# A two-layer graph network on one core: the second layer's products move into the tile of the gathered features, with two such tiles instead of four

## The chip, the cores and the metric

The kernel runs on one core of a Trainium2 chip. The metric is the device time of one execution in microseconds (us), the median of several runs. A difference of about 0.2% is what a measurement of this kernel can tell from none.

## What is computed

The reference takes 6250 nodes with 128 features and 206,250 directed edges sorted by their target node (`dst`). The first layer is a graph attention layer with a feed-forward block; the second, which the change is about, is an equivariant convolution. Cut to what matters, the second layer is:

```python
f0 = x0 @ W1_0e / sqrt(32);  f1 = einsum('nui,uw->nwi', x1, W1_1o) / sqrt(32)
e0, e1 = feat0[edge_src], feat1[edge_src]          # gather by source node
h = gelu(edge_scalar_attr @ W_mlp1 / sqrt(8));  h = gelu(h @ W_mlp2 / sqrt(64))
out0_a = (h @ Wp_00) * e0 * ea0
out0_b = (h @ Wp_11) * sum(e1 * ea1) / sqrt(3)
out1_a = (h @ Wp_01) * e0 * ea1
out1_b = (h @ Wp_10) * e1 * ea0
n0, n1 = segment_sum(concat(out0_a, out0_b)), segment_sum(concat(out1_a, out1_b))   # by dst
y = cos * self + sin * (n0 @ W2_0e, n1 @ W2_1o);   x = layernorm(x + y)
```

Everything is in float32. The output is the 6250 x 128 node table after both layers.

## The kernel before

The edges are cut into tiles of 128 (one edge to a partition), six tiles (TU) make a unit of 768 edges, and there are 269 units. Because edges are sorted, a unit's targets lie in a window of 32 nodes, so its sum over edges is a matmul of the edge values with a one-hot matrix of width 32, and the result is added into an accumulator in SBUF at the unit's first node.

The first layer (`attention`) walks through the units; GpSimd (POOL) gathers one 128-row tile of a node table per instruction (`gather`, line 366), six to a unit. Its output goes into a DRAM table `FEAT` (features for the second layer) and `BASE`.

The second layer is `convolution`, line 746. It works on pairs of units (135 pairs, 134 of two units and one of one), and each pair in three chunks (c = 0, 1, 2), each of two tiles from either unit, so of four edge tiles. The order of the instructions on each engine is the order in which the Python code issues them; waits between engines follow from the buffers. The steps:

- `load(p)`, line 775: SyncE starts the transfers of the edge attributes (`e8` for eight pairs at once, `e4` for each pair).
- `fetch(p)`, line 785: twelve gathers from `FEAT` into the tile `f` of the pair, 128 partitions x 12 x 128 floats. There are four such buffers. The six tiles of the first unit come first, then those of the second; tile t of unit i lies in slot 2t + i, so chunk c reads slots 4c to 4c + 3.
- `radial(p, k)`, line 791: one of the two small dense layers per edge on TensorE (line 801), with a gelu on ScalarE (line 802). It runs two pairs ahead.
- `filters(p, c)`, line 804: the four weights of each edge, on TensorE into PSUM (line 808), two chunks ahead.
- `products(p, c)`, line 810, all on VectorE: `oh`, the one-hot of the targets (line 817); `os`, the one-hot times the four edge attributes (line 823); `vy`, the features times the weights in two versions j, in one multiplication at line 828 and two at line 832. `os` and `vy` come from a pool with two buffers each.
- `sums(p, c)`, line 838: for each of the four edge tiles two matmuls into the PSUM tile `y` of the pair, with `vy` as the weights and `os` as the moving operand (lines 849 and 851).
- `collect(p)`, line 853: VectorE adds `y` to the accumulator, once for each unit (line 859).
- `nodes.step` advances `finish` (line 889) in groups of two blocks of 128 nodes: 16 matmuls (line 908), VectorE and ScalarE work for the norm (`moments`, lines 620 to 623; `norm`, lines 629 to 632), and the store of the output.

The main loop, line 869, goes over steps q = 3p + c. In each: on c = 0 `load(p + 2)` and `fetch(p + 2)`; then `products` of chunk q, `collect` of the pair before on c = 1, `sums` of chunk q - 1, `filters` of chunk q + 2, a `radial` of pair p + 2, and a step of `finish`. In this layer GpSimd has no other instruction than the gathers, after clearing the accumulator at the start (line 761). Before a gather may write into a buffer of `f`, the products of the pair that used it four pairs ago must be done.

Of the kernel before, what the change touches and what calls it, by code (L numbers as in the profile page):

```python
# [8 lines left out]
F32 = mybir.dt.float32  # L9
# [7 lines left out]
P = 128  # L17
D = 128
# [16 lines left out]
TU = 6  # L35
# [72 lines left out]
class Fast:  # L108
# [637 lines left out]
    def convolution(self):  # L746


        tc, nc, a, NU = self.tc, self.nc, self.a, self.NU
        NPR, CT = -(-NU // 2), 2  # L750
        PARTS = TU // CT
        with ExitStack() as st:
            def pool(n, b, **k):
                return st.enter_context(tc.tile_pool(name=n, bufs=b, **k))
            cw, ld, wk = pool("fcw", 1), pool("fcl", 3), pool("fck", 2)
            hp, wp, yp = pool("fhp", 2, space=PSUM), pool("fwp", PARTS, space=PSUM), pool("fyp", 1, space=PSUM)

            acc = cw.tile([P, 4, self.NX], F32, name="acc4")
            step = -(-self.NX // 4)
            for x in range(0, self.NX, step):  # L760
                nc.gpsimd.memset(acc[:, :, x:min(x + step, self.NX)], 0.0)
            nodes = Queue(self.finish(st, yp, acc), self.done)
            m1 = cw.tile([P, EB, P], F32, name="m1")
            nc.scalar.dma_start(m1, a["m1"])
            m2 = cw.tile([P, P], F32, name="m2")
            nc.scalar.dma_start(m2, a["m2"])
            wq = cw.tile([P, 2 * D], F32, name="wq")
            nc.scalar.dma_start(wq, a["wq"])
            fs, e8s, e4s, hs, h1s, ws, vys, ys = {}, {}, {}, {}, {}, {}, {}, {}
            NQ = PARTS * NPR  # L770

            def units(p):
                return min(2, NU - 2 * p)

            def load(p):
                if p % EB == 0:
                    g = min(EB, NPR - p)
                    e8 = ld.tile([P, UE], F32, name="e8", bufs=2)
                    nc.sync.dma_start(e8[:g * 16], a["e8t"][p:p + g].rearrange("g k e -> (g k) e"))
                    for i in range(g):  # L780
                        e8s[p + i] = e8[:g * 16], m1[:g * 16, i]
                e4s[p] = ld.tile([P, 2 * TU, 4], F32, name="e4", bufs=4)
                nc.sync.dma_start(e4s[p], a["e4t"][:, p * 2 * TU:(p + 1) * 2 * TU, :])

            def fetch(p):
                f = fs[p] = ld.tile([P, 2 * TU, D], F32, name="f", bufs=4)
                for i in range(units(p)):
                    for t in range(TU):
                        self.gather(f[:, 2 * t + i, :], self.FEAT, 2 * p + i, t)

            def radial(p, k):


                if k == 0:
                    (x, m), sc = e8s.pop(p), 1.0 / math.sqrt(8.0)
                else:
                    x, m, sc = h1s.pop(p), m2, 1.0 / 8.0
                h = (h1s, hs)[k][p] = wk.tile([P, UE], F32, name=f"h{k}")
                for s in (slice(0, UE // 2), slice(UE // 2, UE)):
                    ps = hp.tile([P, UE // 2], F32, name="h_ps")  # L800
                    nc.tensor.matmul(ps, m, x[:, s], start=True, stop=True)  # L801
                    nc.scalar.activation(h[:, s], ps, AF.Gelu_apprx_tanh, scale=sc)  # L802

            def filters(p, c):
                w = ws[p, c] = wp.tile([P, 2 * CT, D], F32, name="w")
                for t in range(CT):
                    e = (c * CT + t) * P
                    nc.tensor.matmul(w[:, 2 * t:2 * t + 2, :], hs[p][:, e:e + P], wq, start=True, stop=True)  # L808

            def products(p, c):  # L810
                m = units(p)
                own = slice(0, 2 * CT, 3 - m)
                at = slice(2 * CT * c, 2 * CT * (c + 1), 3 - m)
                n = m * CT
                f, w = fs[p][:, at], ws.pop((p, c))[:, own]
                oh = wk.tile([P, CT, 2, W], F32, name="oh")
                nc.vector.tensor_tensor(  # L817
                    oh[:, :, :m],
                    self.l[:, 2 * p:2 * p + m, c * CT:(c + 1) * CT].rearrange("p u t -> p t u")[:, :, :, None]
                    .to_broadcast([P, CT, m, W]),  # L820
                    self.iota[:, None, None, :].to_broadcast([P, CT, m, W]), op=OP.is_equal)
                os = wk.tile([P, 2 * CT, 4, W], F32, name="os")
                nc.vector.tensor_mul(  # L823
                    os[:, own], oh.rearrange("p t u w -> p (t u) w")[:, own, None, :].to_broadcast([P, n, 4, W]),
                    e4s[p][:, at, :, None].to_broadcast([P, n, 4, W]))

                vy = wk.tile([P, 2 * CT, 2, D], F32, name="vy")
                nc.vector.tensor_mul(  # L828
                    vy[:, own, :, :32], w[:, :, :64].rearrange("p t (j x) -> p t j x", j=2),
                    f[:, :, None, :32].to_broadcast([P, n, 2, 32]))  # L830
                for j in range(2):
                    nc.vector.tensor_mul(  # L832
                        vy[:, own, j, 32:].rearrange("p t (c x) -> p t c x", c=3),
                        w[:, :, None, 64 + j * 32:96 + j * 32].to_broadcast([P, n, 3, 32]),
                        f[:, :, 32:].rearrange("p t (c x) -> p t c x", c=3))
                vys[p, c] = os, vy

            def sums(p, c):


                m = units(p)
                os, vy = vys.pop((p, c))
                if c == 0:
                    ys[p] = yp.tile([P, 2, 4, W], F32, name="y", bufs=2)
                for t in range(CT):
                    for i in range(m):
                        e = 2 * t + i
                        last = c == PARTS - 1 and t == CT - 1 and i == m - 1
                        nc.tensor.matmul(ys[p][:, i, 0], vy[:, e, 0], os[:, e, 3],  # L849
                                         start=(c == t == i == 0), stop=False)  # L850
                        nc.tensor.matmul(ys[p][:, i, 1:], vy[:, e, 1], os[:, e, :3], start=False, stop=last)  # L851

            def collect(p):
                y = ys.pop(p)
                for i in range(units(p)):
                    u = 2 * p + i
                    r = nc.vector.value_load(self.r0[0:1, u:u + 1], min_val=0, max_val=self.n)  # L857
                    v = acc[:, :, bass.ds(r, W)]
                    nc.vector.tensor_add(v, v, y[:, i])  # L859

            for p in range(min(2, NPR)):
                load(p)
                fetch(p)
                radial(p, 0)
                radial(p, 1)
            for q in range(2):
                filters(q // PARTS, q % PARTS)

            for q in range(NQ + PARTS):
                p, c = q // PARTS, q % PARTS  # L870
                if c == 0 and p + 2 < NPR:
                    load(p + 2)
                    fetch(p + 2)
                if q < NQ:
                    products(p, c)
                if c == 1 and p:
                    collect(p - 1)
                if 0 < q <= NQ:
                    sums((q - 1) // PARTS, (q - 1) % PARTS)
                if q + 2 < NQ:  # L880
                    filters((q + 2) // PARTS, (q + 2) % PARTS)
                if c != 1 and p + 2 < NPR:
                    radial(p + 2, c // 2)
                if p:
                    nodes.step(min(2 * p, NU) - 1)
            nodes.rest()
# [746 lines left out]
```

## Time and profile before

| | us |
|---|---|
| median of 3 runs | 4422.91 (4422.65 to 4431.17) |
| profiled execution, its own time | 5622.66 |
| its span, first to last instruction | 5620.2 |
| first `f` gather starts, last one starts | 2820.9, 5574.1 |
| POOL busy; `f` gathers, `xl` gathers | 3239.3; 1543.2, 1651.8 |
| PE busy; weight loads | 3763.6; 2955.2 |
| VectorE busy, ScalarE busy | 2550.7, 951.4 |
| mean granted clock of TensorE | 0.742 of full speed |

The page of the profile gives the busy time of each engine (PE is TensorE's matmuls, PEld its weight loads, DVE VectorE, ACT ScalarE, POOL GpSimd, SP SyncE). A group of instructions is a line of the code, an engine, an operation and the tiles, out<-in, with the count, busy us, mean ns of one, the engine's idle time before it and what ended most of that. A wait named "issue" is time in which an engine waited for nothing that the profile shows. A row of the timeline is start, duration, engine, line, operation, tiles and count, and in brackets the idle time before and its releaser. The second layer is about the second half of the profiled span. The profiled execution is longer than the runs that are timed, so its shares are not those of the timed runs.

### The profile page before, as it was taken

The page shows a single profiled execution, that of the slowest core. Times are in us where ns is not written, and L with a number is a line of the kernel's source. Part 1 is how long each engine was busy: PE and PEld are TensorE (multiplying, and loading weights), DVE is VectorE, ACT ScalarE, POOL GpSimd, SP SyncE. Part 2 cuts the span into 40 slices and gives each one's busy share as a digit, 9 for nine tenths or more (in the row PEclk, how much of TensorE's full clock was granted, in tenths as well). Part 3 has the DMA queues.
Part 4 walks back from the last instruction along what each step waited for, and adds up shares of the span by engine and source line. Part 5 has one row for each costly group of instructions (what it writes and reads, how often), then busy time and mean ns, then how long its engine had stood idle before and what let it go on. Part 6 is the DMA issues. An engine that isn't in the chain of part 4 may idle for free. (4 is left out here: it accounts for less than half of the span.)

```text
span 5620.2 us, 66997 instructions
## 1 busy us (share of the span) xinstructions
PE 3763.6 (67%) x21381; PEld 2955.2 (53%) x21381; DVE 2550.7 (45%) x6023; ACT 951.4 (17%) x2528; POOL 3239.3 (58%) x3236
## 2 busy tenths in 40 slices
PE   3566667667767676666656767767766766676667
PEld 2455555555555555545534555555555655555556
DVE  1465555656655656655623333333333333333334
ACT  1111212222221222212301111111111111111111
POOL 6256666666666666664255555555555555655553
PEclk6677777777777777776767777777777777777778
DMA  4444344334443444433111111111111111111111
GB/s 118 133 117 110 106 108 117 107 105 119 115 110 107 113 112 112 111 100 100 41 50 44 44 47 43 46 42 44 46 46 44 44 46 42 47 46 46 46 43 32
DMA packets 290616, 428.21 MB, mean 76 GB/s; under 512 B 122700, under 2 KB 199454, under 8 KB 290254
## 3 DMA queue, kind: packets, MB, share of 16 engines
q0 software_dynamic: 103296, 218.27, 15.9%
q1 hardware_dynamic: 183258, 197.74, 11.8%
q10 hardware_dynamic: 3700, 7.82, 0.4%
q8 instruction: 173, 2.83, 0.2%
q14 instruction: 189, 1.55, 0.1%
HBM read 403.55 MB, written 19.96 MB: 75 GB/s over the span
## 5 line engine op out<-in xcount | busy, mean ns | idle before, releaser
L366 POOL DMA_INDIRECT f<-fFEAT,fsrc x1614 | 1543.2, 956 | 1225.6 <-DVE oh L817 620.4
L366 POOL DMA_INDIRECT xl<-fXL,fsrc x1590 | 1651.8, 1039 | 989.4 <-issue 422.5
L823 DVE TENSOR_TENSOR os<-oh,e 128x512 f32<-128x512 f32 x405 | 280.3, 692 | 1543.1 <-remote 689.6
L851 PE MATMUL y<-os,vy 128*128 128x96 f32 x3228 | 794.6, 324 | 249.4 <-issue 247.6
L849 PEld LDWEIGHTS y<-os,vy 128*128 128x128 f32 x3228 | 590.5, 214 | 398.0 <-issue 267.3
L849 PE MATMUL y<-os,vy 128*128 128x32 f32 x3228 | 588.8, 260 | 275.4 <-issue 225.8
L420 PE MATMUL z<-fw,ea 128*128 128x136 f32 x3228 | 661.5, 351 | 137.3 <-issue 63.1
L851 PEld LDWEIGHTS y<-os,vy 128*128 128x128 f32 x3228 | 562.7, 214 | 248.3 <-issue 247.3
L420 PEld LDWEIGHTS z<-fw,ea 128*128 128x128 f32 x3228 | 561.2, 244 | 205.5 <-issue 117.3
L802 ACT ACTIVATE h<-h_ps 128x384 f32<-128x384 f32 x540 | 259.4, 490 | 2415.4 <-remote 985.3
L808 PE MATMUL w<-wq,h 128*128 128x256 f32 x1620 | 549.7, 456 | 113.3 <-issue 99.4
L538 PE MATMUL m<-xl,oh 128*32 128x136 f32 x3228 | 267.5, 352 | 272.3 <-issue 98.2
L808 PEld LDWEIGHTS w<-wq,h 128*128 128x128 f32 x1620 | 329.1, 223 | 196.7 <-issue 167.8
L832 DVE TENSOR_TENSOR vy<-w,f 128x384 f32<-128x384 f32 (+1 forms) x810 | 408.3, 545 | 0.0
L801 PE MATMUL h_ps<-e,m 128*128 128x384 f32 (+1 forms) x540 | 265.2, 624 | 202.4 <-ACT h L802 172.0
L551 PEld LDWEIGHTS m<-fcst,sb 128*128 128x128 f32 x1076 | 193.0, 237 | 341.7 <-issue 159.0
L551 PE MATMUL m<-fcst,sb 128*128 128x32 f32 x1076 | 183.4, 302 | 210.5 <-ACT sb L543 109.1
L423 PE MATMUL z<-xl,fcst 128*128 128x408 f32 x538 | 306.5, 655 | 13.7 <-issue 12.5
L538 PEld LDWEIGHTS m<-xl,oh 128*32 128x32 f32 x3228 | 132.9, 127 | 340.4 <-issue 141.8
L801 PE MATMUL h_ps<-h,m 128*128 128x384 f32 x540 | 258.1, 595 | 41.6 <-issue 41.1
L528 DVE TENSOR_TENSOR xl<-xl,ex 128x384 f32<-128x384 f32 x538 | 274.1, 550 | 8.8 <-ACT ex L511 8.8
L801 PEld LDWEIGHTS h_ps<-e,m 128*128 128x128 f32 (+1 forms) x540 | 125.2, 241 | 290.7 <-ACT h L802 198.4
(145 smaller groups left out, 4242.7 us busy)
## 6 DMA issues: line engine op xcount, KB each, us to landing
ea<-fast_eat_dram SPq DMA_DIRECT2D x269, 384.0 KB
lb<-fLB SPq DMA_DIRECT2D x269, 144.0 KB
f<-fFEAT,fsrc POOLq DMA_INDIRECT x1614
xl<-fXL,fsrc POOLq DMA_INDIRECT x1590
xr<-fXR SPq DMA_DIRECT2D x807, 8.5 KB
e<-fast_e8t_dram SPq DMA_DIRECT2D x16, 384.0 KB
fXR<-pt SPq DMA_DIRECT2D x16, 306.0 KB
fXL<-tb SPq DMA_DIRECT2D x16, 204.0 KB
```

Source lines behind the costliest of these rows:

```text
L366: self.nc.gpsimd.indirect_dma_start(out=to, out_offset=None, in_=table, in_offset=bass.IndirectOffsetOnAxis(ap=self.src[:, g:g + 1], axis=0))
L420: nc.tensor.matmul(z[:, t * ZW:(t + 1) * ZW], lhs[:, e], rhs, start=(t == 0 and lhs is ea), stop=(half == 1 and t == 2 and lhs is oht))
L423: nc.tensor.matmul(z, self.ident, xl[:, :3, :].rearrange("p t f -> p (t f)"), start=False, stop=True)
L528: nc.vector.tensor_mul(v, v, ws[b][0][:, t:t + 3, i * H:(i + 1) * H, None].to_broadcast([P, 3, H, O]))
L538: nc.tensor.matmul(ag[q * W:(q + 1) * W], oh[:, t, :], xl[:, t, :], start=(t < 4), stop=(t + 4 >= TU))
L551: nc.tensor.matmul(nd[:, i, j], sb[:, j], self.s4, start=True, stop=True)
L801: nc.tensor.matmul(ps, m, x[:, s], start=True, stop=True)
L808: nc.tensor.matmul(w[:, 2 * t:2 * t + 2, :], hs[p][:, e:e + P], wq, start=True, stop=True)
L823: nc.vector.tensor_mul(os[:, own], oh.rearrange("p t u w -> p (t u) w")[:, own, None, :].to_broadcast([P, n, 4, W]), e4s[p][:, at, :, None ...
L832: nc.vector.tensor_mul(vy[:, own, j, 32:].rearrange("p t (c x) -> p t c x", c=3), w[:, :, None, 64 + j * 32:96 + j * 32].to_broadcast([P, ...
L849: nc.tensor.matmul(ys[p][:, i, 0], vy[:, e, 0], os[:, e, 3], start=(c == t == i == 0), stop=False)
L851: nc.tensor.matmul(ys[p][:, i, 1:], vy[:, e, 1], os[:, e, :3], start=False, stop=last)
```

## The change

The tile `f` becomes three times as wide: 12 slots x 3 x 128 floats, with the gathered features in the third part of a slot and the products of that edge tile in the first two. The separate `vy` tile is gone, and `sums` reads its weights from `f`. There are two such tiles instead of four: 36 KB a partition, where four `f` and two `vy` took 32 KB. Since a tile now holds what TensorE reads, a gather into it waits until the sums of the pair two before are done. `fetch` moves: for pairs from 2 on it is issued one pair ahead instead of two, in the step c = 0 of pair p for pair p + 1, after the `sums` of the last chunk of pair p - 1. The twelve gathers of a pair go tile by tile, both units in turn, so slot after slot. `load` keeps its place.

```diff
             def fetch(p):
-                f = fs[p] = ld.tile([P, 2 * TU, D], F32, name="f", bufs=4)
-                for i in range(units(p)):
-                    for t in range(TU):
-                        self.gather(f[:, 2 * t + i, :], self.FEAT, 2 * p + i, t)
+                f = fs[p] = ld.tile([P, 2 * TU, 3, D], F32, name="f", bufs=2)
+                for t in range(TU):
+                    for i in range(units(p)):
+                        self.gather(f[:, 2 * t + i, 2, :], self.FEAT, 2 * p + i, t)
...
-                f, w = fs[p][:, at], ws.pop((p, c))[:, own]
+                fv, w = fs[p][:, at], ws.pop((p, c))[:, own]
+                f, vy = fv[:, :, 2], fv[:, :, :2]
...
-                vy = wk.tile([P, 2 * CT, 2, D], F32, name="vy")
                 nc.vector.tensor_mul(
-                    vy[:, own, :, :32], w[:, :, :64].rearrange("p t (j x) -> p t j x", j=2),
+                    vy[:, :, :, :32], w[:, :, :64].rearrange("p t (j x) -> p t j x", j=2),
                     f[:, :, None, :32].to_broadcast([P, n, 2, 32]))
                 for j in range(2):
                     nc.vector.tensor_mul(
-                        vy[:, own, j, 32:].rearrange("p t (c x) -> p t c x", c=3),
+                        vy[:, :, j, 32:].rearrange("p t (c x) -> p t c x", c=3),
...
-                os, vy = vys.pop((p, c))
+                os, vy = oss.pop((p, c)), fs[p][:, 2 * CT * c:2 * CT * (c + 1)]
...
                 if c == 0 and p + 2 < NPR:
                     load(p + 2)
-                    fetch(p + 2)
                 if q < NQ:
                     products(p, c)
                 if c == 1 and p:
                     collect(p - 1)
                 if 0 < q <= NQ:
                     sums((q - 1) // PARTS, (q - 1) % PARTS)
+                if c == 0 and 0 < p < NPR - 1:
+                    fetch(p + 1)
                 if q + 2 < NQ:
                     filters((q + 2) // PARTS, (q + 2) % PARTS)
```

## The prediction

> **What bounds the kernel now.** I read the page's busy times and groups first, then the waits, the timeline in the second layer (about 2820 to 5620 us of the span), and the busy times by stretch.
>
> Busy times and two groups of the page (busy us, mean ns | idle before, releaser):
>
> ```profile
> PE 3763.6 (67%) x21381; PEld 2955.2 (53%) x21381; DVE 2550.7 (45%) x6023; ACT 951.4 (17%) x2528; POOL 3239.3 (58%) x3236
> L366 POOL DMA_INDIRECT f<-fFEAT,fsrc x1614 | 1543.2, 956 | 1225.6 <-DVE oh L817 620.4
> L366 POOL DMA_INDIRECT xl<-fXL,fsrc x1590 | 1651.8, 1039 | 989.4 <-issue 422.5
> ```
>
> The waits (us in total, times, longest):
>
> ```profile
> POOL f L366 <- DVE oh L817: 620.4, 75, 17.7
> POOL f L366 <- issue: 466.4, 1502, 2.4
> POOL xl L366 <- issue: 422.5, 1363, 2.1
> PEld y L849 <- issue: 267.3, 301, 3.5
> PE y L851 <- issue: 247.6, 234, 2.6
> PE y L849 <- issue: 225.8, 227, 3.2
> DVE vy L828 <- DMA f<-fFEAT,fsrc: 12.2, 1, 12.2
> ```
>
> In this profiled execution the second layer is paced by PE. POOL runs ahead until all four `f` buffers are full and then waits for products; products waited for a gather once, at the very start. But much of PE's pace is not work: it waits for nothing the profile shows. Single matmuls stand some 2 us apart although everything is there:
>
> ```profile
> 2867.89 0.21 PE L849 MATMUL y<-os,vy 128*128 128x32 f32 x1 [2.84 <-issue]
> 2869.99 0.21 PE L849 MATMUL y<-os,vy 128*128 128x32 f32 x1 [1.89 <-issue]
> 2872.79 0.32 PE L851 MATMUL y<-os,vy 128*128 128x96 f32 x1 [2.59 <-issue]
> ```
>
> POOL is steady throughout, 0.94 us a gather and 0.30 between:
>
> ```profile
> 2829.65 0.94 POOL L366 DMA_INDIRECT f<-fFEAT,fsrc  x1 [0.30 <-issue]
> 2830.89 0.94 POOL L366 DMA_INDIRECT f<-fFEAT,fsrc  x1 [0.30 <-issue]
> 2832.30 0.43 DVE L828 TENSOR_TENSOR vy<-w,f 128x256 f32<-128x256 f32 x1 [12.20 <-DMA f<-fFEAT,fsrc]
> ```
>
> The profiled execution took 5622.7 us (span 5620.2, so 2.5 around it), the median of the runs is 4422.9: 1200 us less. So I asked which engine cannot shrink. A gather costs 0.956 + 466.4/1614 = 1.245 us in the second layer and 1.039 + 422.5/1590 = 1.305 in the first. POOL's sum: 58.5 (start of the first `xl` gather) + 1590 x 1.305 = 2075 + 137.5 (last `xl` gather to first `f` gather) + 1614 x 1.245 = 2010 + 45 (last gather to the end) = 4326 us. That is 97.8% of the median: without the recording, POOL's gathers bound the kernel nearly throughout, and the second layer takes between 14.94 us a pair of units (12 gathers) and 15.7 (if all the missing 97 us lie in its 134.5 pairs).
>
> PE's work per pair, from the timeline in two stretches: at full speed four edge tiles' sums took 1.76 us (4010.81 to 12.57), a chunk's filters 1.06, a radial step 1.45: 3 x 1.76 + 3 x 1.06 + 2 x 1.45 = 11.4, with 0.3 for `finish` 11.7 us. At half speed 3.36 (3999.77 to 4003.13), 1.97 and 2.77: 22 us. The mean over the layer was in between:
>
> ```profile
> 4000.00:4600.00 600.00, 416.56 (x2124) 338.17 (x2123) 213.88 (x547) 78.73 (x148) 332.75 (x348) 0.76 0.17 45
> ```
>
> (PE, PEld, DVE, ACT, POOL busy, granted clock, DMA share, GB/s.) So PE has room under 14.9 us when it runs full, and none at half.
>
> **What the Trainium skill says.** "TensorE: Matmul & The Clock Gate", Part 1: the array has two clocks, half and full, and one busy window of about 3.4 us releases the full one. The trace agrees in kind: sums at 3.36 or 1.76 us a chunk, 0.742 granted on average. A PE that falls behind is busy, so it should get its full clock back; that self-correction carries my forecast. "DMA: Bandwidth & Descriptors", SWDGE vs HWDGE vs iDMA: gathers issued from GpSimd have their descriptors made by its own cores in software. The trace agrees: POOL is busy 0.94 us for each and does nothing else here, so its cadence is a floor. "SBUF — State Buffer", Who interferes with whom: a DVE operation with two SBUF inputs can block a GpSimd one that reads SBUF. The trace shows little: `f` gathers average 956 ns against a median of 944, 1614 x 0.012 = 19 us in all.
>
> **The change, part by part.**
> (1) Products go into the tile of the features. Same three multiplications (0.42 + 2 x 0.505 = 1.43 us), same element counts, other strides with the same inner rows: 0. If the stride did cost, DVE does 7.8 us of a pair (3 x 2.4 + 0.6), so even 1 us a pair is covered by POOL's 14.9.
> (2) The `vy` buffer and its wait go. Nothing is gained: `os` still has two buffers, is written just before, and waits for the same sums (`DVE os L823 <- PE y L851` in the waits, 248 us). 0.
> (3) Gathers tile by tile. Same 1614 gathers and the same waits for eight earlier ones. Products of chunk 0 need 4 gathers (5.0 us) instead of 8 (10.0), chunk 1 needs 8 instead of 10, chunk 2 all 12 in both. Where POOL is the bound, only the end can gain. I take 1 to 3 us.
> (4) Two tiles instead of four, and `fetch(p+1)` after the last sums of p-1. This is the new wait: the first gather of a pair now waits for PE. Queued behind it on POOL are only gathers; `load` and its SP transfers stay where they were. The added semaphore wait is taken by the sequencer while the gather before still runs: 0. Who waits for the gathers is DVE's products, behind them `collect`, then PE.
>
> When does (4) bite? Call G the end of a pair's last gather. It lands 1.7 us later (a gather started at 2829.65 released products at 2832.30: 2.65 after its start, 1.7 after its end). Products take 1.4, then PE may first finish filters and a radial step (0 to 2.5 us full, 4.7 half), then sums 1.76 (3.36 half). So the last sums end at G + 4.9 to 7.4 at full clock, up to 11.2 at half. POOL meanwhile has the next pair's 12 gathers to do, to G + 14.9. POOL stalls only if PE is another 7.5 to 10 us late at full clock (3.7 at half). I expect no regular stall: 0 us a pair.
>
> Against the profiled execution itself the sum is also 0. Over the layer I took, pair by pair from the timeline, the time from a pair's last sums to the products two pairs later: chunk 0 median 16.6 us, least 7.2, where 4 gathers and landing need 3.75 + 2.65 = 6.4; chunk 1 median 22.7, least 11.2, needed 11.4; chunk 2 median 32.5, least 14.0, needed 16.4. Only 2 of 131 pairs would be late, by under 9 us together. So the profiled span should stay within 1% of 5620, and the runs at 4423 - 1 = 4422.
>
> **Rivals.** Slower: PE's lateness eats the smaller lead. Before, POOL could be three pairs (45 us) ahead, now one. The place is a `finish` group: 16 matmuls (2.15 us full), two activation table loads (1.28 us each), DVE waiting for ACT at line 629 (61.6 us in 22 waits, 2.8 each), with PE perhaps at half clock, where it loses 22 - 14.9 = 7 us a pair. It decides once a pair's last sums end more than 14.9 us after its last gather; what is lost then is never regained, since POOL is the bound. At 2.5 us lost for each of 25 groups: 62 us, 4485; at half of that 4454. If PE were at the profile's 0.75 clock all along (14.7 us busy a pair), 5% of the layer, 100 us, could go. For it: half clock is frequent here. Against it: that clock comes with the pauses above.
>
> Faster: the smoother arrival. Products start 5 us earlier in each pair, PE is less bunched, the tail ends some 5 us sooner, and if gathers then met DVE less, up to the 19 us of collisions go: 4423 - 24 = 4399. Against it: nothing in the middle waits for the first chunk while POOL is the bound.
>
> The change does not do what it says: if a tile were tracked as a whole, products would wait for all 12 gathers and gathers for products, some 26 us a pair and 5900 us. In the waits of the changed program each product waits for four gathers only, so 1 in 100, counted with slower.
>
> **How the numbers follow.** No change measurable (within 0.2%, 9 us, about what a measurement here can tell): 0.50, at 4422. Slower: 0.32, mostly 4435 to 4490, a tail to 4530. Faster: 0.18, 4399 to 4413. The range 4406 to 4485 leaves out about 0.07 below and 0.12 above.
>
> **What would show it.** In the profile after: POOL waits for `y` on PE at the head of a pair instead of for `oh`; 1614 gathers at about 950 ns; products wait for gathers a little at most; span near 5620. The forecast fails if products' waits for gathers reach tens of us, if the gathers' idle time grows while PE's pauses do not, or if the time leaves the bound of POOL's sum, which would mean that another engine had set the pace.

## The result, and the profile after

The changed kernel takes 4409.6 us (median of 6 runs, 4404.8 to 4420.1), the kernel before 4422.8 (6 runs): ratio 0.997, 95% interval [0.9956, 0.9983], 13 us faster. The profiled execution of 5622.7 us shown above matches a chip on which TensorE pauses without a cause that the profile shows: there the timed runs of the kernel before take 5617 us as well. So it was most likely the chip, and not the recording, that made that profile longer. Every time below is compared with the kernel before on the same chip; the profiles set side by side come from several chips without the pauses.

The page of the changed kernel, profiled on a chip without the pauses (its own time 4420.1 us, span 4418.2), the busy times and the two groups of gathers. Its line numbers in the second layer are up to three higher than before: `os` is line 825, the products 829 and 833, the sums 850 and 852.

```profile
PE 3545.6 (80%) x21381; PEld 2843.6 (64%) x21381; DVE 2581.9 (58%) x6023; ACT 963.3 (22%) x2528; POOL 3333.3 (75%) x3236
L366 POOL DMA_INDIRECT xl<-fXL,fsrc x1590 | 1711.8, 1077 | 487.3 <-issue 401.9
L366 POOL DMA_INDIRECT f<-fFEAT,fsrc x1614 | 1577.2, 977 | 506.5 <-issue 443.7
```

Its waits (us in total, times, longest):

```profile
DVE f L829 <- DMA f<-fFEAT,fsrc: 973.2, 404, 3.8
POOL f L366 <- issue: 443.7, 1456, 0.3
PEld y L850 <- DVE f L833: 301.5, 218, 2.9
DVE os L825 <- PE y L852: 26.7, 26, 2.0
```

POOL does not wait for any buffer here: its longest pause between two `f` gathers is 0.3 us, whatever the profile names as its cause. VectorE waits for gathers in 404 of 405 chunks, and TensorE for VectorE. That is what a layer paced by POOL looks like; the waits lead back to the gathers. Of the pauses named "issue" before the matmuls in `sums`, 15 us in all are left, none over 0.3.

To compare, the kernel before was profiled twice on such chips (among the experiments below). The first of these profiles, the same lines:

```profile
PE 3546.7 (80%) x21381; PEld 2915.5 (66%) x21381; DVE 2569.7 (58%) x6023; ACT 963.4 (22%) x2528; POOL 3321.3 (75%) x3236
L366 POOL DMA_INDIRECT xl<-fXL,fsrc x1590 | 1694.2, 1066 | 487.3 <-issue 399.5
L366 POOL DMA_INDIRECT f<-fFEAT,fsrc x1614 | 1582.6, 981 | 506.8 <-issue 423.9
```

```profile
DVE vy L828 <- DMA f<-fFEAT,fsrc: 847.1, 204, 12.1
POOL f L366 <- issue: 423.9, 1391, 0.3
DVE os L823 <- PE y L851: 160.3, 92, 3.0
```

The same picture: before the change POOL was the bound already, and four buffers gave it nothing that two do not. What differs on POOL in this layer is the gathers' own duration. From the timelines of the runs on such chips (the one with a single tile left out) I took POOL's time apart (us):

| kernel | last `xl` to first `f` gather | first to last `f` gather | `f` gathers busy | `f` gathers over 1.0 us | last gather to end |
|---|---|---|---|---|---|
| before, first profile | 93.6 | 2074.2 | 1582.6 | 168 | 18.6 |
| before, second profile | 88.7 | 2076.0 | 1584.4 | 157 | 19.5 |
| order only | 87.7 | 2066.8 | 1575.0 | 137 | 18.4 |
| changed, first profile | 88.4 | 2068.8 | 1577.2 | 153 | 19.6 |
| changed, again | 93.7 | 2065.4 | 1573.8 | 157 | 19.3 |
| changed, one-hot in PSUM | 89.9 | 2018.1 | 1526.2 | 0 | 19.8 |
| the same again | 89.9 | 2014.6 | 1523.0 | 0 | 19.5 |
| before, one-hot in PSUM | 107.4 | 2014.5 | 1522.8 | 0 | 20.3 |

The pauses between the `f` gathers sum to 491.6 to 491.9 us in each of these. From the first to the last gather the kernel before needs 2075.1 us on average, the changed one 2067.1, and the 8.0 us between them are the gathers' busy time (1583.5 against 1575.5). These are two profiles of each, and they differ by up to 3.4 us among themselves. On the one chip where both kernels were profiled, the step is 8.8 us (2074.2 against 2065.4).

Why gathers differ in length shows in the timeline of the changed kernel; here VectorE's `os` and the gathers around it:

```profile
3403.22 0.69 DVE L825 TENSOR_TENSOR os<-oh,e 128x512 f32<-128x512 f32 x1
3403.37 1.36 POOL L366 DMA_INDIRECT f<-fFEAT,fsrc  x1 [0.30 <-issue]
...
3407.53 0.94 POOL L366 DMA_INDIRECT f<-fFEAT,fsrc  x1 [0.30 <-issue]
...
3408.09 0.69 DVE L825 TENSOR_TENSOR os<-oh,e 128x512 f32<-128x512 f32 x1
...
3408.78 0.94 POOL L366 DMA_INDIRECT f<-fFEAT,fsrc  x1 [0.30 <-issue]
```

A gather that begins while `os` runs (3403.37) takes 1.36 us instead of 0.94. One that `os` joins later (3407.53, joined at 3408.09), or that begins as `os` ends (3408.78), takes 0.94. The loss depends on how much of `os` is left: a gather that begins 0.1 to 0.2 us after it takes 1.31 to 1.41 us, one that begins 0.4 to 0.5 us after it 1.01 to 1.10. In this trace all 153 gathers over 1.0 us overlap an `os`; 147 begin in it, 6 in the `oh` just before it.

The Trainium skill ("SBUF — State Buffer", Who interferes with whom) says that a VectorE operation with two inputs in SBUF contends with a GpSimd operation that reads SBUF, that the port which they share is an exclusive lock, and that the order of issue decides which of the two is blocked. The measurement agrees that the gather is held when `os` is first: `os` reads `oh` and `e4` from SBUF, the gather its row numbers `fsrc`. In the other order no hold is seen: an `os` that begins during a gather takes at most 0.71 us. The same section reports that a `tensor_tensor`, the operation of `os`, did not stall a DMA in the test it tells of, and infers a reason; these gathers are stalled.

Where the order helps can be read by chunk. The gathers that begin in the `oh` or `os` of the first chunk of a pair lose 13.5 and 18.4 us in the two profiles before (the excess over 0.944 us each), and 6.1 to 7.1 us in the three with the new order and `os` in SBUF. The second chunk loses 8.7 and 10.1 us before and 7.4 to 9.8 after, the third 32.8 to 37.3 and 34.8 to 37.8. So the gain on POOL sits in the first chunk, the one whose products the new order releases after four gathers instead of eight. The waits of `os` for sums fall as well, from 160.3 us to 26.7. That this is the step between order and collisions is likely, but not shown.

### The profile page after: what moved, and what is told of

Read it like the earlier page. It is cut to its first block, busy times and chain, and to the rows that moved or that the text cites. A ratio compares the mean times of both kernels' runs of the same rounds, so it can differ in the third digit from the quotient of the medians.

```text
span 4418.2 us, 67000 instructions
## 1 busy us (share of the span) xinstructions
PE 3545.6 (80%) x21381; PEld 2843.6 (64%) x21381; DVE 2581.9 (58%) x6023; ACT 963.3 (22%) x2528; POOL 3333.3 (75%) x3236
## 3 DMA queue, kind: packets, MB, share of 16 engines
q0 software_dynamic: 103296, 218.27, 20.3%
## 4 chain that ended last, share of the span: by engine, by line
POOL 31%; DMA 20%; PE 20%; issue 15%; DVE 11%; ACT 1%; DVEq 1%; ACTq 0%; SPq 0%; POOLq 0%
POOL f L366 21%; DMA xl<-fXL,fsrc 10%; POOL xl L366 9%; DMA f<-fFEAT,fsrc 8%; PE z L420 6%; PE z L423 3%; DVE f L833 2%; PE m L538 2%; PE y L852 2%; PE m L551 1%; DVE f L829 1%; DVE pr L439 1%; DVE os L825 1%; PE y L850 1%; DVE xl L528 1%
## 5 line engine op out<-in xcount | busy, mean ns | idle before, releaser
L366 POOL DMA_INDIRECT xl<-fXL,fsrc x1590 | 1711.8, 1077 | 487.3 <-issue 401.9
L366 POOL DMA_INDIRECT f<-fFEAT,fsrc x1614 | 1577.2, 977 | 506.5 <-issue 443.7
L852 PE MATMUL y<-os,f 128*128 128x96 f32 x3228 | 774.8, 325 | 10.2
L850 PEld LDWEIGHTS y<-os,f 128*128 128x128 f32 x3228 | 551.3, 208 | 353.2 <-DVE f L833 301.5
L829 DVE TENSOR_TENSOR f<-w,f 128x256 f32<-128x256 f32 x405 | 171.6, 424 | 982.0 <-DMA f<-fFEAT,fsrc 973.2
L850 PE MATMUL y<-os,f 128*128 128x32 f32 x3228 | 583.5, 264 | 198.1 <-DVE f L833 197.7
L852 PEld LDWEIGHTS y<-os,f 128*128 128x128 f32 x3228 | 538.5, 209 | 31.5 <-DVE f L833 30.6
L809 PE MATMUL w<-wq,h 128*128 128x256 f32 x1620 | 498.3, 437 | 0.0
L833 DVE TENSOR_TENSOR f<-w,f 128x384 f32<-128x384 f32 (+1 forms) x810 | 408.7, 546 | 0.0
L423 PEld LDWEIGHTS z<-xl,fcst 128*128 128x128 f32 x538 | 99.6, 231 | 390.2 <-issue 316.3
L825 DVE TENSOR_TENSOR os<-oh,e 128x512 f32<-128x512 f32 x405 | 280.2, 692 | 64.6 <-PE y L852 26.7
L436 DVE TENSOR_TENSOR pr<-z,xl 128x408 f32<-128x408 f32 x269 | 154.7, 575 | 209.9 <-DMA xl<-fXL,fsrc 117.7
L445 DVE TENSOR_REDUCE lg<-pr 128x48 f32<-128x816 f32 x269 | 266.5, 991 | 1.8 <-DVE pr L439 1.8
```

The source lines that it names most:

```text
L366: self.nc.gpsimd.indirect_dma_start(out=to, out_offset=None, in_=table, in_offset=bass.IndirectOffsetOnAxis(ap=self.src[:, g:g + 1], axis=0))
L423: nc.tensor.matmul(z, self.ident, xl[:, :3, :].rearrange("p t f -> p (t f)"), start=False, stop=True)
L445: nc.vector.tensor_reduce(lgs[b][:, :, i * H:(i + 1) * H], prs.pop(u).rearrange("p (t h) o -> p t h o", h=H), axis=mybir.AxisListType.X, o ...
L825: nc.vector.tensor_mul(os[:, own], oh.rearrange("p t u w -> p (t u) w")[:, own, None, :].to_broadcast([P, n, 4, W]), e4s[p][:, at, :, None ...
L833: nc.vector.tensor_mul(vy[:, :, j, 32:].rearrange("p t (c x) -> p t c x", c=3), w[:, :, None, 64 + j * 32:96 + j * 32].to_broadcast([P, n, ...
L850: nc.tensor.matmul(ys[p][:, i, 0], vy[:, e, 0], os[:, e, 3], start=(c == t == i == 0), stop=False)
```

## The experiments

The theory after the result: POOL paces both kernels, the shorter lead costs nothing, and the 13 us are fewer or shorter collisions of gathers with `os`, brought by the order of the gathers. Rivals: the gain lies in the shared tile or the late `fetch`; it lies at the end of the layer; the lead is nearly used up, so that the next step to shorten it costs; and PE is the bound after all.

**Four runs on a chip with the pauses.** There the kernel before takes 5616.9 us.

The kernel before, unchanged:

> The kernel before, unchanged, once more, for a profile in which PE is not slowed by pauses without a cause: a control. POOL theory: ratio 1.000 within 0.2%; in the second layer no wait of POOL for a buffer, gathers 0.30 us apart, as in the changed kernel. The changed kernel was 13 us faster; if that is fewer collisions of gathers with the one-hot product os on VectorE, the f gathers of this run average about 985 ns against 977 (13 us over 1614), with more of them over 1300 ns. If it is the end of the layer, the time from the last gather's end to the last instruction is about 13 us longer than the 19.6 us of the changed kernel. If it is PE's pace after all, POOL shows waits for products of some 13 us in all.

5618.8 us, ratio 0.9995 [0.9974, 1.0016]. The pauses were there, in timed runs and profile alike (the profiled execution took 5602.2 us), so this run says nothing on the theory.

The order alone:

```diff
-                for i in range(units(p)):
-                    for t in range(TU):
+                for t in range(TU):
+                    for i in range(units(p)):
                         self.gather(f[:, 2 * t + i, :], self.FEAT, 2 * p + i, t)
```

> Of the change only the gathers' order, tile by tile for both units; four f buffers and a separate vy as before. If the gain is the order (smoother arrival, another phase of VectorE's os against the gathers), it is here in full: 4408 to 4413 us, ratio 0.997, f gathers near 977 ns. If it is the shared tile or the shorter lead that does it, ratio 1.000, 4423 us. The rival that a longer lead is worth something would have this one faster than the changed kernel.

5620.9 us, 1.0008 [0.9981, 1.0034]: nothing, where POOL does not set the pace.

The change without its order:

```diff
-                for t in range(TU):
-                    for i in range(units(p)):
+                for i in range(units(p)):
+                    for t in range(TU):
                         self.gather(f[:, 2 * t + i, 2, :], self.FEAT, 2 * p + i, t)
```

> The changed kernel with its gathers unit by unit again; two shared tiles, late fetch. Products of the first chunk then need 8 gathers instead of 4, so the three chunks of a pair arrive within 5 us and the last sums end some 4 to 8 us later after the last gather (about 10 to 14 us against a lead of 15.4). If the lead still suffices, 4423 us, ratio 1.000, POOL without waits; if it is just used up, POOL waits for y on PE in part of the pairs, 1 to 3 us each, 4450 to 4700 us. The order theory of the gain says not faster than before.

5415.0 us, 0.9644 [0.9606, 0.9682]. 200 us faster, which neither theory expected. The waits of the kernel before on this chip, then of this one, both from 2850 to 5380 us:

```profile
POOL f L366 <- DVE oh L817: 516.7, 80, 17.3
PEld y L849 <- issue: 241.8, 289, 11.8
PE y L851 <- issue: 216.8, 233, 2.6
```

```profile
POOL f L366 <- PE y L852: 246.8, 44, 13.9
PEld y L850 <- issue: 197.4, 292, 4.0
PE y L852 <- issue: 169.0, 190, 2.6
```

POOL waits for sums as the change intends, and PE's pauses without a cause sum to less. From the first to the last `f` gather the layer takes 2478 us against 2682. Why a POOL held back by PE should ease PE's pauses, these records don't tell; the changed kernel itself was not run on this chip. Nor was the change without its order run on a chip without the pauses, so its other parts are tested there only by leaving them out (the run of the order alone below).

One tile instead of two, so no lead; in the first step of a pair the sums come ahead of the gathers:

```diff
-                f = fs[p] = ld.tile([P, 2 * TU, 3, D], F32, name="f", bufs=2)
+                f = fs[p] = ld.tile([P, 2 * TU, 3, D], F32, name="f", bufs=1)
...
-                fetch(p)
+                if p == 0:
+                    fetch(p)
...
+                if c == 0 and 0 < q <= NQ:
+                    sums((q - 1) // PARTS, (q - 1) % PARTS)
+                if c == 0 and 0 < p < NPR:
+                    fetch(p)
                 if q < NQ:
                     products(p, c)
                 if c == 1 and p:
                     collect(p - 1)
-                if 0 < q <= NQ:
+                if c and 0 < q <= NQ:
                     sums((q - 1) // PARTS, (q - 1) % PARTS)
-                if c == 0 and 0 < p < NPR - 1:
-                    fetch(p + 1)
```

> The changed kernel with one shared tile: gathers of a pair wait for the last sums of the pair just before, and in the first step of a pair the sums are issued ahead of the gathers and the products. The lead is gone, so the lateness shows in full: a pair takes 12 gathers (15.4 us) plus the time from the last gather to the end of the last sums (median 6.0 us in the changed kernel's trace) plus up to 1 us to start again: 134 x 6 to 7 = 800 to 940 us more than the changed kernel, 5210 to 5350 us. If gathers were not the bound but PE (11.7 us of work a pair at full clock), part of it would be hidden and the loss below 400 us.

5810.7 us, 1.0339 [1.0292, 1.0387]: 194 us slower. That fits the last sentence of the expectation: where PE sets the pace, much of the lateness is hidden. The 5210 to 5350 meant a chip without pauses; it is run there below.

**Two runs on a chip without the pauses.** The changed kernel once more, and one profiled execution of the kernel before:

> The changed kernel, once more, beside the kernel before on the same chip. Two cases. On a chip where the kernel before takes 4423 us, POOL sets the pace: 4410 us, ratio 0.997, POOL without waits for a buffer. On a chip where PE pauses without a cause and the kernel before takes 5617 us, the kernel with the order undone took 5415 us: if the shared tile with its shorter lead is what eases the pauses, this one is near 5415 too, ratio 0.96 to 0.97; if the unit-by-unit order was needed for it, nearer 5617, ratio 1.00.

> The kernel before, for its profile on the same chip. Where the time is 4423 us: f gathers 0.30 us apart with hardly a wait, so POOL is the bound there already; their mean about 985 ns if the 13 us of the changed kernel are collisions with VectorE's os (977 there), or about 977 ns and some 13 us more between the last gather and the end if they are the tail. Where it is 5617 us: POOL waits over 500 us for products, as in the runs seen so far.

4406.5 us against 4418.2, ratio 0.9963 [0.9949, 0.9977]: the gain is repeated. The profile of the kernel before (a single execution of 4412.8 us, shorter than its median and than the changed kernel's profiled one of 4416.1) shows POOL without a wait and gathers of 980.6 ns; the changed kernel has 975.1. The end is not longer (18.6 us against 19.3), so the tail is out.

**Three runs on another chip without them.** The one-hot in PSUM. `ps` of `finish` had a PSUM bank to itself; it shares it with `oh` and a copy of `iota`, so that `oh` and `os` have one input in SBUF and one in PSUM each:

```diff
-            nodes = Queue(self.finish(st, yp, acc), self.done)
+            px = yp.tile([P, 512], F32, name="px")
+            nodes = Queue(self.finish(st, px, acc), self.done)
...
+            iop = px[:, 384:384 + W]
+            nc.vector.tensor_copy(iop, self.iota)
...
-                oh = wk.tile([P, CT, 2, W], F32, name="oh")
+                oh = px[:, 256:384].rearrange("p (t u w) -> p t u w", t=CT, u=2)
...
-                    self.iota[:, None, None, :].to_broadcast([P, CT, m, W]), op=OP.is_equal)
+                    iop[:, None, None, :].to_broadcast([P, CT, m, W]), op=OP.is_equal)
...
-            ps = yp.tile([P, G, D], F32, name="ps")
+            ps = px[:, :G * D].rearrange("p (g d) -> p g d", g=G)
```

> The changed kernel, with VectorE's one-hot oh and its ruler iota in PSUM instead of SBUF, so that neither of the two one-hot products has two inputs in SBUF; same instructions and counts. In the changed kernel 154 of 1614 f gathers took over 1.0 us, where seen beside os. If gathers meeting os and oh are what the seconds-layer time over the cadence is made of, the f gathers' mean falls from 975 to 977 ns to about 946 and the time by 1614 x 0.030 = 48 us, to about 4360 us against 4420 before, ratio 0.986. If the slow gathers have another cause (the DMA queue, HBM), the mean stays near 976 and the time near 4408. Where PE pauses and the kernel before takes 5617 us, no such gain is seen.

4363.3 us against 4428.0, ratio 0.9855 [0.9837, 0.9873]. The group of its page, and three rows of its timeline:

```profile
L366 POOL DMA_INDIRECT f<-fFEAT,fsrc x1614 | 1526.2, 946 | 506.6 <-issue 439.4
```

```profile
3403.75 0.69 DVE L828 TENSOR_TENSOR os<-px,e 128x512 f32<-128x512 f32 x1 [0.44 <-issue]
3404.11 0.94 POOL L366 DMA_INDIRECT f<-fFEAT,fsrc  x1 [0.30 <-issue]
3405.36 0.94 POOL L366 DMA_INDIRECT f<-fFEAT,fsrc  x1 [0.30 <-issue]
```

A gather now begins in the middle of `os` and takes 0.94 us. In this trace 230 gathers begin in an `os`, all take 0.94 or 0.95 us, and no gather is over 1.0 us. The collisions in time are still there and cost nothing; so what made gathers slow was the second SBUF input of `os` and `oh`, and in this layer it cost the changed kernel some 50 us. `os` itself is as long as before, 0.69 us. This version beats both kernels.

The order alone, here:

> Of the change only the gathers' order; four f buffers, separate vy, early fetch. Where POOL is the bound: if the changed kernel's 12 to 13 us come from the other phase of VectorE's work against the gathers (all products follow the landing of four gathers), they are here too: about 4408 us, ratio 0.997, f gathers' mean near 976 ns, last sums about 6 us after the last gather. If they come from the shared tile or the late fetch, ratio 1.000 and a mean near 981. Where PE pauses: ratio 1.00, as seen.

4415.5 us against 4428.0, ratio 0.9969 [0.9959, 0.9979]: as much as the whole change gained, with four buffers and a separate `vy`. The shared tile and the late `fetch` are worth nothing that these measurements can tell.

```profile
L366 POOL DMA_INDIRECT f<-fFEAT,fsrc x1614 | 1575.0, 976 | 506.2 <-issue 473.1
```

One tile, here:

> The changed kernel with one shared tile; gathers of a pair wait for the last sums of the pair before. Where POOL is the bound: a pair takes 12 gathers (15.35 us) plus the lateness, 4.8 to 9.2 us in the changed kernel's trace (median 6.0), plus up to 1 us to start again, since nothing else fills POOL: 134 x 6 to 7.5, so 800 to 1000 us more, 5210 to 5410 us. If PE were the real bound of the layer, much of the lateness would be hidden: below 4800 us. Where PE pauses: 5811 us, as seen.

5262.4 us, ratio 1.1885 [1.1863, 1.1906], 834 us slower than the kernel before and inside the 5210 to 5410 expected. The wait that the lead had covered now stands in the list, and in the timeline at the head of a pair:

```profile
DVE f L829 <- DMA f<-fFEAT,fsrc: 1847.8, 405, 10.9
PEld y L850 <- DVE f L833: 893.2, 266, 7.1
POOL f L366 <- PE y L852: 882.8, 134, 9.1
```

```profile
3403.53 0.44 PE L852 MATMUL y<-os,f 128*128 128x96 f32 x2
3404.25 0.94 POOL L366 DMA_INDIRECT f<-fFEAT,fsrc  x1 [7.36 <-PE y L852]
3405.49 0.95 POOL L366 DMA_INDIRECT f<-fFEAT,fsrc  x1 [0.30 <-issue]
```

134 waits, 6.6 us each: the lateness of the sums, in full. The rival that a shorter lead costs is real; it sets in between one tile and two.

**Three runs on one more.** The same PSUM edit on the kernel before, the changed kernel with it again, and a second profile of the kernel before:

> The kernel before (four f buffers, separate vy, gathers unit by unit) with the one-hot oh and its ruler in PSUM, as in the run on the changed kernel. If the changed kernel's whole gain of 12 to 13 us is collisions of gathers with os, there is nothing left to gain once they are gone: the same time as the changed kernel with PSUM within 3 us (about 4363), f gathers' mean 946 ns. If part of the gain came from the earlier first chunk by another way (the start or the end of the layer), this one is 5 to 6 us slower than that one. Where PE pauses and the kernel before takes 5617 us: ratio 1.00 within 0.3%.

> The changed kernel with the one-hot in PSUM, again, beside the former on the same chip: 4363 us where POOL is the bound. Where PE pauses, the shared tiles with their shorter lead may ease the pauses as they did with the order undone: then near 5415 us, ratio 0.96 to 0.97; if that took the unit-by-unit order, ratio 1.00.

> The kernel before, one more profile, for the spread of the collisions: where POOL is the bound, an f gathers' mean of 981 to 985 ns (the look before had 981) and 18 to 19 us from the last gather to the end.

The changed kernel with PSUM: 4360.6 us, 0.9855 [0.9836, 0.9874], as before. The kernel before with PSUM: 4377.1, 0.9898 [0.9881, 0.9915], 16 us slower: not within 3, and not the 5 to 6 either. The traces say where the difference is: not in the layer, whose gathers take the same 2014.5 and 2014.6 us (the last two rows of the table), but ahead of it, 107.4 us against 89.9. That the gathers need the same time once nothing slows them is the second half of the evidence: on POOL, in this layer, the two kernels differ by collisions alone. In the timeline of the kernel before with PSUM, the constants of `finish` are scaled while POOL clears the accumulator, in the middle of the last node groups of the first layer:

```profile
2286.01 16.17 POOL L761 MEMSET acc<- 128x6304 f32 x3
2286.71 4.80 DVE L900 TENSOR_SCALAR w2ab<-w2ab 32x128 f32<-32x128 f32 x1
2291.54 0.25 DVE L680 RECIPROCAL iv<-iv 128x16 f32<-128x16 f32 x1
2291.83 5.06 DVE L900 TENSOR_SCALAR w2ab<-w2ab 32x128 f32<-32x128 f32 x1
```

These are the second and third of three scalings; the first took 3.85 us. With the changed kernel's tiles the three take 0.70 us together, after the clearing:

```profile
2310.80 0.70 DVE L903 TENSOR_SCALAR w2ab<-w2ab 32x128 f32<-32x128 f32 x3 [2.09 <-DMA w2ab<-fast_w2ab_dram]
```

The early scalings take 13 us longer. ScalarE, too, turns to the second layer's gelus while node groups of the first are still to do, and loads its activation tables 14 times in this stretch (18.0 us) instead of 8 times (10.3). The kernels' tiles lie elsewhere in SBUF, so it is likely that the transfer of `w2ab` no longer had to wait for a tile of the first layer; that is argued, not shown. In the two profiles of the kernel before, the scalings come after the clearing and that stretch takes 93.6 and 88.7 us, as in the changed kernel, so it is no part of the change's gain. The second of these profiles (4417.2 us) gave gathers of 981.7 ns, as expected, and a tail of 19.5 us, half a microsecond over the forecast.

## Why the prediction was right, and where not

Its range, 4406 to 4485, held 4409.6, but 3.6 us above its lower end. Its likeliest case, no change, did not come true: the gain of 0.3% is clear of noise. It is the size of the rival "faster" (4399 to 4413, given 0.18). So the account of what bounds the kernel and of the lead was right, and that the range held the gain as well was in part luck.

- **What bounds the kernel: right, for a wrong reason.** POOL's gathers set the pace in both kernels, without a pause over 0.32 us between two gathers of one layer. But "without the recording" failed: on each chip the profiled execution takes about as long as the timed runs. Whether the changed kernel would stay "within 1% of 5620" on a chip with the pauses was not run; the nearest to it, the change without its order, took 5415 us there.
- **Its signs.** It named tens of us of products' waiting for gathers as a sign that it fails. They wait 973 us, and 847 us in the kernel before. That is what a layer paced by gathers looks like, and costs nothing, because they wait for the bound. The sign was read from a profile in which PE set the pace. For the same reason POOL does not wait for `y` at the head of a pair, as was forecast.
- **POOL's sum, 4326 us: close in total, wrong in its terms.** Measured in the first profile before: 45.4 + 2178.5 + 93.6 + 2074.2 + 18.6 = 4410.3. The fixed parts were 83 us smaller. The cadences were larger, 1.370 and 1.285 us instead of 1.305 and 1.245, for two reasons. The sum counted only the pauses named "issue" but spread them over all gathers; the pause is 0.305 us after every gather, in the prediction's own profile too, which makes some 87 us. And the gathers themselves were longer, 0.981 us instead of 0.956 for `f` and 1.066 instead of 1.039 for `xl`, which makes 82 us. So the 97 us that its sum missed are not stalls of POOL in the second layer; there are none.
- **The lead: right.** From a pair's last gather to the end of its last sums it had 4.9 to 7.4 us at full clock, up to 11.2 at half; measured 4.9 to 9.2 (5th to 95th percentile over 134 pairs, median 6.0, longest 10.6), below the 14.7 to 15.4 that the next pair's gathers last. The kernel before has 6.3 to 11.5 (median 9.2): the new order also makes the last sums earlier. Landing was put at 1.7 us: products began 1.6 to 2.0 us after the last gather's end. The one-tile run shows what this lead covers, 6.6 us a pair.
- **PE's clock: not tested.** The forecast leaned on a late PE getting its full clock back. PE was never late enough for that: from 2400 to 4200 us it was granted 0.86 to 0.89 in the two profiles of the changed kernel and 0.84 to 0.85 in those before, and it stayed inside the lead. The slower rival's 14.7 us of PE a pair do not come out of the numbers beside it; the profile that it names has 1872.9 us of PE over 134.5 pairs, 13.9 each.
- **The shared tile, the `vy` buffer, the added semaphore: right at 0.** The order alone gives as much as the change.
- **The order, part (3): here it failed.** "Where POOL is the bound, only the end can gain. I take 1 to 3 us." The end did not gain (18.6 and 19.5 us before, 19.3 and 19.6 after). The step overlooked that the order also sets when VectorE works against the gathers, so it changes the bound's own duration. The rival "faster" had this mechanism, with the wrong size twice: the excess over the median gather is 59 and 61 us before, not 19, because 19 was read from the profile with PE's pauses, in which 85 gathers were over 1.0 us and not 157 or 168; and the change takes away 5 to 11 us of it, not all.
- **What stays open.** The gathers' time explains about 8 of the 12 to 13 us between the medians. The interval of the first comparison begins at 7.5 us, those of the repeat and of the order alone at 10.2 and 9.3, so a few us may have another source. It can't be read from the profiles: the first layer, the same instructions in each of these kernels, varies from 2178 to 2196 us, and the profiled executions as a whole (spans of 4410.4 and 4415.4 us before, 4418.2 and 4413.9 after) do not show the gain that the medians show. On the chip with pauses neither their cause nor the 200 us are explained, and whether they belong to that chip or to a state it was in is not known.

## What to carry to other kernels

Before you shorten a lead, measure how late its slowest consumer is behind the producer. Here the lead beyond that lateness could be given away for nothing, and the next step less cost the lateness in full at each turn. Where an engine is the bound, look at the spread of its own instructions, not only at its waits: here a tenth of the gathers were slow, nearly all beside one operation of another engine, and ending that was worth some 50 us, when four tiles instead of two were worth nothing. And compare a profile with a timed run of the same chip before you explain the difference.

## What the runs showed of the hardware that was not expected

- A gather issued on POOL that begins during a VectorE multiplication with both inputs in SBUF is lengthened by up to 0.5 us (0.94 to 1.46); with one input in PSUM it is not (0 of 1614 over 1.0 us, against 137 to 168).
- A gather that is already running when that multiplication begins is not lengthened, and neither is the multiplication (at most 0.71 us, against 0.69).
- Three VectorE scalings that take 0.70 us together took 3.85, 4.80 and 5.06 us beside POOL's clearing of SBUF.
- One chip ran the kernel before in 5617 us and three others in 4418 to 4428, at a mean granted clock of 0.74 and 0.82, with gathers equally long where they were profiled (median 944 to 947 ns).
